# Layer 2's exponentials and piece scalings pinned to source order on ScalarE, reciprocal rows kept through SyncE's queue

## The chip, the cores and the metric

The kernel runs on one core of a Trainium2 chip. The metric is the device time of one launch in microseconds (us); the time before is the median of three runs. Engines carry the names of the profile: PE is TensorE (PEld its weight loads), DVE VectorE, ACT ScalarE, POOL GpSimd, SP SyncE. A q behind a name (SPq, ACTq, POOLq) is the sequencer of that engine, which waits and issues transfers. L967 is line 967 of the kernel.

## The reference, cut to what matters

Four layers follow each other on `x` of shape (4, 512, 32, 32): four images, 512 channels, 1024 positions. Each layer is `x = x + layer(groupnorm(x))`. Layers 0 and 3 (attention with mixed heads, and a memory read with the top 8 of 2048 items) are not touched. Layer 1 is a gate for each channel. Layer 2, which the change touches, is plain attention with eight heads of 64:

```python
def _L2_conv_ref(x, Wq, bq, Wkv, bkv, Wp, bp):
    q = _conv1x1(x, Wq, bq)
    kv = _conv1x1(x, Wkv, bkv)
    k, v = jnp.split(kv, 2, axis=1)
    q, k, v = (t.reshape(b, NUM_HEADS, D_K, l) for t in (q, k, v))   # shortened
    attn = jnp.einsum('bhct,bhcs->bhts', q, k) * SCALE
    attn = jax.nn.softmax(attn, axis=-1)
    out = jnp.einsum('bhts,bhcs->bhct', attn, v)
    out = _conv1x1(out.reshape(b, c, h, w), Wp, bp)
    return out

# --- layer 1 ---
x = x + _L1_conv_ref(_gn(x), ...)        # a gate for each channel of each image
# --- layer 2 ---
x = x + _L2_conv_ref(_gn(x), L2_conv_Wq, L2_conv_bq, L2_conv_Wkv, L2_conv_bkv, L2_conv_Wp, L2_conv_bp)
```

The kernel computes the softmax without taking off a maximum. Every reciprocal of a sum of exponentials is kept, and at the end of the kernel all of them are tested against two bounds; if one lies outside, a slower general path computes the result again.

## The kernel before, the parts concerned

The language places instructions by a scheduler that works with a model of their durations: an instruction without a mark goes where the model finds its inputs ready and its engine free, even far ahead of its place in the source. The kernel's helper `pin` takes that freedom away for one instruction: it goes behind whatever was written last for the same engine.

```python
    def pin(ins):
        return tc.keep_in_program_order(ins)
```

Layer 2 works in units. A unit is a pair of heads `m`, a half of the queries `n` and four of the eight tiles of keys: 16 units for an image, 64 in all. `scores2` multiplies keys by queries into PSUM (L973), ScalarE takes the exponentials (L967), and `apply2` multiplies the unit before with its values (L1006). The exponentials are added up on GpSimd (L987, L991) and VectorE (L992).

```python
    def scores2(b, u, before=None):
        ...
        def exp2():
            e = places2[:, count[0] % 6]
            count[0] += 1
            nc.scalar.activation(e, scs[len(es)], AF.Exp)                 # L967
            es.append(e)

        for i, t in enumerate(range(t0, t0 + 4)):
            sc = ps_s.tile([P, 2, NB], F32, tag="sc", ...)                # three such buffers
            for r in range(2):
                pin(nc.tensor.matmul(sc[:, r, :], ...k..., ...q..., start=True, stop=True))  # L973
            scs.append(sc)
            if before is None or i < 2:
                exp2()
        if before is not None:
            apply2(b, before, exp2)      # values of the unit before; takes the other two exp2 inside
        ...
        nc.gpsimd.tensor_add(I["es", m, n], es[0], es[1])                 # L987, first half of the keys
        ...
            nc.gpsimd.tensor_add(two, es[i], es[i + 1])                   # L991
            nc.vector.tensor_add(I["es", m, n], I["es", m, n], two)       # L992
```

When both halves of the keys are done, `finish2` sums the exponentials over the partitions by a matmul with ones, takes the reciprocal and scales the output. The last two lines keep one row of reciprocals for each of the two heads, for the test at the end.

```python
    def finish2(b):
        ...
            pin(nc.tensor.matmul(rsp[r * HD:(r + 1) * HD, :], ones[:, 0:HD], es[:, r, :], ...))   # L1027
        ri = apool.tile([P, NB], F32, tag="rb", bufs=2, name=f"ri_{nm}")
        nc.scalar.copy(ri, rsp)                                           # L1032
        nc.vector.reciprocal(ri, ri)                                      # L1033
        nc.vector.tensor_mul(I["o"][:, m, n * NB:(n + 1) * NB], pv, ri)   # L1034
        for r in range(2):
            i = 2 * ((b * KC + m) * (T // NB) + n) + r
            nc.gpsimd.dma_start(out=seen[i:i + 1, :], in_=ri[r * HD:r * HD + 1])   # L1037
```

`put_out2` projects the output of an image and adds the image itself, gated by layer 1. That image lies in DRAM; eight pieces of it (`xr`, 128 x 512, in two buffers) are loaded, scaled by ScalarE, added to the projection by VectorE and stored.

```python
    def put_out2(b):
        ...
        def add_out(m, ps):
            for n in range(T // NB):
                xr = apool.tile([P, NB], F32, tag="xr", bufs=2, name=f"xr_c{b}_{m}_{n}")
                nc.sync.dma_start(out=xr, in_=x1[b][:, m, n * NB:(n + 1) * NB])        # L1048
                nc.scalar.activation(xr, xr, AF.Identity,
                                     bias=I["tb"][:, m:m + 1], scale=s1[:, m:m + 1])   # L1049
                nc.vector.tensor_add(xr, ps[:, n * NB:(n + 1) * NB], xr)               # L1051
                nc.sync.dma_start(out=x2[b][:, m, n * NB:(n + 1) * NB], in_=xr)        # L1052
                nc.vector.bn_stats(st[:, n, :], xr)
        for m in range(KC):
            project(I["Wp"], tokens(I["o"]), m, None, lambda ps: add_out(m, ps), f"p2_{b}")   # matmuls at L197
```

Around an image the source says this:

```python
    scores2(0, UNITS2[0])
    for b in range(B):
        for s, u in enumerate(UNITS2):
            if s >= 1:
                scores2(b, u, UNITS2[s - 1])
            ...   # two steps of `behind` (layer 1's gate, norms) and of `ahead` (the next image), each unit
        ...       # take_q2 of the next image
        apply2(b, UNITS2[-1])
        ...       # take_k2
        finish2(b)
        ...       # take_v2
            scores2(b + 1, UNITS2[0])
        put_out2(b)
```

The gate of the last image is computed beside layer 2's first units. Some of its small steps go back and forth between TensorE and GpSimd:

```python
        def turned(l, products):
            products(ps)                               # small matmuls, pinned: L836, then L841 and L842
            take_small(u, ps[:, 0:KC])                 # ScalarE, L133
            yield
            for i in range(2):
                for n in range(2):
                    nc.gpsimd.tensor_scalar_mul(us[:, n], u, a_)                       # L829
                nc.gpsimd.tensor_sub(u_v[:, :, 0], cos_v[:, :, 0], sin_v[:, :, 1])     # L832
                nc.gpsimd.tensor_add(u_v[:, :, 1], cos_v[:, :, 1], sin_v[:, :, 0])     # L833
            return u
```

Of the kernel before, what the change touches and what calls it, by code (L numbers as in the profile page):

```python
# [11 lines left out]
AF = mybir.ActivationFunctionType  # L12
# [12 lines left out]
HD = C // NH  # L25
# [16 lines left out]
def fast_net(ctx: ExitStack, tc: tile.TileContext, a: dict, out: bass.AP, flag: bass.AP):  # L42
    nc = tc.nc
# [12 lines left out]
    def pin(ins):  # L56

        return tc.keep_in_program_order(ins)
# [21 lines left out]
    fcw, seen = both[0:NQ], both[HD:P]  # L80
# [5 lines left out]
    for i in range(P // NH):  # L86
        nc.scalar.dma_start(
            out=whp[i * NH:(i + 1) * NH], in_=a["w_head"].rearrange("r m g -> (r m) g")
# [13 lines left out]
        out=gavg_v, in_=gavg_v, compare_op=ALU.is_ge, fill=0.0, base=0,  # L102
# [3 lines left out]
        out=gavg_v, in_=gavg_v, compare_op=ALU.is_ge, fill=0.0, base=GSZ - 1,  # L106
# [81 lines left out]
    def tokens(src):  # L188
        return lambda k, n: src[:, k, n * NB:(n + 1) * NB]

    def project(w, rhs, m, at, evacuate, name="proj"):


        ps = place(at, f"{name}_{m}")
        for n in range(T // NB):
            for k in range(KC):
                pin(nc.tensor.matmul(  # L197
                    ps[:, n, :], w[:, k, m * P:(m + 1) * P], rhs(k, n),
                    start=(k == 0), stop=(k == KC - 1),
                ))  # L200
        evacuate(flat2(ps))
# [33 lines left out]
    e = apool.tile([P, 2, 2, 2, NK], F32, tag="e", name="e")  # L235
# [719 lines left out]
    def scores2(b, u, before=None):  # L955

        m, n, t0 = u
        I = img[b]  # L960
        nm = f"c{b}_{m}_{n}"
        es, scs = [], []

        def exp2():
            e = places2[:, count[0] % 6]
            count[0] += 1
            nc.scalar.activation(e, scs[len(es)], AF.Exp)  # L967
            es.append(e)

        for i, t in enumerate(range(t0, t0 + 4)):  # L970
            sc = ps_s.tile([P, 2, NB], F32, tag="sc", name=f"sc_{nm}_{t}")
            for r in range(2):
                pin(nc.tensor.matmul(  # L973
                    sc[:, r, :],
                    I["k"][r * HD:(r + 1) * HD, m, t * P:(t + 1) * P],
                    I["q"][r * HD:(r + 1) * HD, m, n * NB:(n + 1) * NB],
                    start=True, stop=True,
# [5 lines that stand above are left out]
            apply2(b, before, exp2)  # L983
        I["e", u] = list(es)
        if t0 == 0:
            I["es", m, n] = sums2[:, (2 * m + n) % 2]
            nc.gpsimd.tensor_add(I["es", m, n], es[0], es[1])  # L987
            es = es[2:]
        for i in range(0, len(es), 2):
            two = pair_sum[:, (t0 + i) // 2 % 2]  # L990
            nc.gpsimd.tensor_add(two, es[i], es[i + 1])  # L991
            nc.vector.tensor_add(I["es", m, n], I["es", m, n], two)  # L992

    def apply2(b, u, exp2=None):

        m, n, t0 = u
        I = img[b]
        if t0 == 0:
            finish2(b)
            I["pv", m, n] = ps_m.tile([P, NB], F32, tag="mm", name=f"pv_c{b}_{m}_{n}")  # L1000
        pv = I["pv", m, n]
        for i, e in enumerate(I.pop(("e", u))):
            t = t0 + i
            for r in range(2):
                h = 2 * m + r
                pin(nc.tensor.matmul(  # L1006
                    pv[r * HD:(r + 1) * HD, :], I["v"][:, t, h * HD:(h + 1) * HD],
                    e[:, r, :], start=(t == 0), stop=(t == TC - 1),
                ))
            if exp2 and i < 2:  # L1010
                exp2()
        if t0 == TC - 4:
            I["due"] = (m, n)

    def finish2(b):
        I = img[b]
        due = I.pop("due", None)
        if due is None:
            return
        m, n = due  # L1020
        nm = f"c{b}_{m}_{n}"
        if due == (0, 0):
            I["o"] = o_full.rearrange("p (k t) -> p k t", k=KC)
        es, pv = I.pop(("es", m, n)), I.pop(("pv", m, n))
        rsp = ps_s.tile([P, 2, NB], F32, tag="sc", name=f"rs_{nm}")[:, 0, :]
        for r in range(2):
            pin(nc.tensor.matmul(  # L1027
                rsp[r * HD:(r + 1) * HD, :], ones[:, 0:HD], es[:, r, :],
                start=True, stop=True,
# [4 lines that stand above are left out]
        nc.vector.tensor_mul(I["o"][:, m, n * NB:(n + 1) * NB], pv, ri)  # L1034
        for r in range(2):
            i = 2 * ((b * KC + m) * (T // NB) + n) + r
            nc.gpsimd.dma_start(out=seen[i:i + 1, :], in_=ri[r * HD:r * HD + 1])  # L1037

    def put_out2(b):
        I = img[b]  # L1040
        s1 = l2[b][1]
        mv = small.tile([P, KC, 2], F32, tag="mv", name=f"mv_d{b}")

        def add_out(m, ps):
            st = small.tile([P, 2, 6], F32, tag="bnst", name=f"st_d{b}_{m}")
            for n in range(T // NB):
                xr = apool.tile([P, NB], F32, tag="xr", bufs=2, name=f"xr_c{b}_{m}_{n}")
                nc.sync.dma_start(out=xr, in_=x1[b][:, m, n * NB:(n + 1) * NB])  # L1048
                nc.scalar.activation(  # L1049
                    xr, xr, AF.Identity, bias=I["tb"][:, m:m + 1], scale=s1[:, m:m + 1])  # L1050
                nc.vector.tensor_add(xr, ps[:, n * NB:(n + 1) * NB], xr)  # L1051
                nc.sync.dma_start(out=x2[b][:, m, n * NB:(n + 1) * NB], in_=xr)  # L1052
                nc.vector.bn_stats(st[:, n, :], xr)
            nc.vector.bn_aggr(mv[:, m, :], st.rearrange("p i s -> p (i s)"))

        for m in range(KC):
            project(I["Wp"], tokens(I["o"]), m, None, lambda ps: add_out(m, ps), f"p2_{b}")
        gc3 = const.tile([P, 2, KC], F32, tag=f"gc3_{b}", name=f"gc3_{b}")
        l3[b] = (mv, gc3)
# [247 lines left out]
    for b in range(B):  # L1307
# [22 lines left out]
        if not last:  # L1330
            for m in range(KC):
                take_k2(b + 1, m)
        finish2(b)
        if last:
            atts[0] = attention(*tiles[0])
# [745 lines left out]
```

## Time and profile before

| | before |
|---|---|
| time, median of 3 runs | 2743.99 us |
| lowest and highest | 2740.64 and 2755.8 us |
| span of the profiled run | 2741.6 us |
| mean granted TensorE clock | 0.980 |
| layer 2 in the profile | about 1373 to 2266 us |
| PE busy from 1590 to 1810 us | 217.44 of 220 us |
| ACT busy there | 77.56 us |
| POOL busy there | 93.16 us |
| DVE busy there | 89.71 us |

The first exponential of layer 2 starts at 1374.6 us and the last scaled piece (L1049) at 2266.1 us. In between one engine, PE, is busy nearly all the time, and the three others less than half of it. In such a stretch the time is made by what PE has to do and by the moments at which PE stands idle; the idle time of the other engines matters only where PE waits for it.

### The profile page before, as it was taken

How to read it: one execution, taken by the hardware profiler on the slowest of the kernel's cores; microseconds unless marked ns; L12 is line 12 of the kernel's file. 1: busy time of each engine (PE TensorE's matmuls, PEld its weight loads, DVE VectorE, ACT ScalarE, POOL GpSimd, SP SyncE). 2: the span in 40 equal slices, each digit the busy share in tenths (PEclk: the TensorE clock that was granted, in tenths of full speed). 3: DMA queues.
4: the chain of work that ended last, by engine and by line, in shares of the span. 5: the costliest groups of instructions: out<-in, count | busy, mean ns of one | idle time of the engine just before them, and what ended most of it. 6: DMA issues, size and time to landing. Idle time of an engine off the chain costs nothing.

```text
span 2741.6 us, 46996 instructions
## 1 busy us (share of the span) xinstructions
PE 2593.0 (95%) x18286; PEld 1180.3 (43%) x18286; DVE 1522.8 (56%) x2386; ACT 1007.6 (37%) x1149; POOL 1266.2 (46%) x1955
## 2 busy tenths in 40 slices
PE   8988999989989898989999999999999999999995
PEld 3443544545445444545433433343343334444442
DVE  5487337871588526873235224513623537788886
ACT  0565336551565426552154025214502622121210
POOL 2266325552455514653067017305702735666664
PEclk9999999999999999999999999999999999999997
DMA  2577438880687627785310030021002016767665
GB/s 78 128 206 204 128 93 219 218 216 28 172 216 202 164 69 193 205 207 199 116 32 1 31 123 1 16 77 62 1 31 92 1 48 189 220 186 216 185 183 148
DMA packets 159321, 349.82 MB, mean 128 GB/s; under 512 B 32361, under 2 KB 65129, under 8 KB 155378
## 3 DMA queue, kind: packets, MB, share of 16 engines
q1 hardware_dynamic: 86304, 167.04, 21.2%
q0 software_dynamic: 51200, 142.93, 19.3%
q10 hardware_dynamic: 21586, 36.76, 4.6%
q8 instruction: 147, 2.41, 0.4%
q14 instruction: 84, 0.69, 0.1%
HBM read 178.57 MB, written 33.69 MB: 77 GB/s over the span
## 4 chain that ended last, share of the span: by engine, by line
PE 82%; DMA 7%; ACT 4%; DVE 2%; issue 1%; POOL 1%; SPq 1%; ACTq 0%; POOLq 0%; DVEq 0%
PE at L1094 16%; PE sc_c L973 7%; PE pv_c L1006 7%; PE sc L451 7%; PE mx L197 7%; PE pv L511 6%; PE pt L410 4%; DMA s<-ss 4%; PE p L197 4%; PE sc L197 4%; PE v L209 3%; PE k L197 3%; PE q L197 3%; PE pt L684 3%; ACT ss L457 2%; PE mx L471 2%
## 5 line engine op out<-in xcount | busy, mean ns | idle before, releaser
L484 DVE STREAM_TRANSPOSE eT<-e 128x1024 f32<-128x1024 f32 x256 | 317.6, 1242 | 273.9 <-ACT e L478 272.0
L464 POOL DMA_DIRECT2D s<-ss x512 | 259.8, 515 | 384.4 <-ACT ss L457 299.6
L1111 POOL DMA_INDIRECT got<-in_mem,ix x256 | 280.2, 1095 | 208.3 <-DVE tmx L1117 92.3
L457 ACT COPY ss<-sc 128x1024 f32<-128x1024 f32 x256 | 258.9, 1011 | 264.4 <-PE sc L451 212.7
L967 ACT ACTIVATE eT<-sc_c 128x1024 f32<-128x1024 f32 x256 | 247.9, 1021 | 275.3 <-PE sc_c L973 213.3
L500 DVE BATCH_NORM_STATS2 st<-e 128x6 f32<-128x256 f32 x1024 | 341.6, 406 | 0.0
L451 PE MATMUL sc<-k,q 64*32 64x512 f32 x4096 | 287.1, 617 | 22.5 <-ACT ss L457 17.6
L991 POOL TENSOR_TENSOR e<-eT 128x1024 f32<-128x1024 f32 x96 | 231.3, 2412 | 164.7 <-ACT eT L967 133.2
L478 ACT ACTIVATE e<-mx 128x1024 f32<-128x1024 f32 x256 | 262.5, 1029 | 65.5 <-PE mx L471 28.0
L992 DVE TENSOR_TENSOR eT<-eT,e 128x1024 f32<-128x1024 f32 x96 | 132.8, 1384 | 274.0 <-POOL e L991 274.0
L511 PE MATMUL pv<-eT,v 128*64 128x128 f32 x4096 | 256.5, 279 | 0.0
L973 PE MATMUL sc_c<-q,k 64*128 64x512 f32 x1024 | 243.2, 614 | 11.3 <-ACT eT L967 9.0
L511 PEld LDWEIGHTS pv<-eT,v 128*64 128x64 f32 x4096 | 226.1, 139 | 63.9 <-issue 62.3
L1006 PE MATMUL pv_c<-eT,v 128*64 128x512 f32 x1024 | 234.4, 600 | 0.0
L471 PE MATMUL mx<-s,wmix 32*32 32x512 f32 x4096 | 159.6, 625 | 45.0 <-DMA s<-ss 44.9
L1135 DVE SCALAR_TENSOR_TENSOR acc<-got,et,acc 128x512 f32<-128x512 f32 x224 | 168.4, 752 | 8.0
L1033 DVE RECIPROCAL ri_c<-ri_c 128x512 f32<-128x512 f32 x32 | 107.0, 3345 | 96.1 <-ACT ri_c L1032 96.1
L973 PEld LDWEIGHTS sc_c<-q,k 64*128 64x128 f32 x1024 | 94.9, 189 | 144.0 <-issue 74.7
L1099 ACT COPY att<-at 128x1024 f32<-128x1024 f32 x64 | 64.8, 1012 | 217.8 <-PE at L1094 217.6
L987 POOL TENSOR_TENSOR eT<-eT 128x1024 f32<-128x1024 f32 x32 | 76.0, 2374 | 147.0 <-ACT eT L967 146.8
L587 POOL TENSOR_TENSOR o<-pv,rb 64x256 f32<-64x256 f32 x128 | 111.1, 868 | 67.1 <-ACT pv L574 60.2
L1006 PEld LDWEIGHTS pv_c<-eT,v 128*64 128x64 f32 x1024 | 70.9, 138 | 155.2 <-issue 154.6
(317 smaller groups left out, 3325.5 us busy)
## 6 DMA issues: line engine op xcount, KB each, us to landing
s<-ss SPq DMA_DIRECT2D x512, 128.0 KB
s<-ss POOLq DMA_DIRECT2D x512, 128.0 KB, 4.4
rb<-r POOLq DMA_DIRECT2D x64, 128.0 KB, 5.9
o<-o SPq DMA_DIRECT2D x32, 256.0 KB
xr<-in_x ACTq DMA_DIRECT2D x32, 256.0 KB
x<-xr SPq DMA_DIRECT2D x32, 256.0 KB
xr_c<-x SPq DMA_DIRECT2D x32, 256.0 KB
x<-xr_c SPq DMA_DIRECT2D x32, 256.0 KB
```

What stands on the lines that cost most here:

```text
L197: pin(nc.tensor.matmul(ps[:, n, :], w[:, k, m * P:(m + 1) * P], rhs(k, n), start=(k == 0), stop=(k == KC - 1),))
L451: pin(nc.tensor.matmul(sc[m * NS:(m + 1) * NS, r, :], q[r * HD:(r + 1) * HD, m, s * NS:(s + 1) * NS], k_[r * HD:(r + 1) * HD, m, n * NB:(n ...
L457: pin(nc.scalar.copy(ss[:, :, n * NB:(n + 1) * NB], sc))
L464: pin(relays[r].dma_start(out=s2[r * KC + m::NH], in_=ss[m * NS:(m + 1) * NS, r, :]))
L478: pin(nc.scalar.activation(e[:, half].rearrange("p r qq k -> p (r qq k)"), flat2(pairs[f"mx{half}"]), AF.Exp))
L484: pin(nc.vector.transpose(eT[:, j % 2].rearrange("p b (qq i r) x -> p i r qq b x", qq=2, i=4)[:, i, 2 * half:2 * half + 2], e[:, half].rea ...
L500: pin(nc.vector.bn_stats(st[:, i, 2 * half + r, qq, :], e[:, half, r, qq, :]))
L511: pin(nc.tensor.matmul(pv[r * HD:(r + 1) * HD, gp, :], I["v"][:, t, g * HD:(g + 1) * HD], eT[:, j % 2, t, :, 4 * g:4 * g + 4], start=(t == ...
L973: pin(nc.tensor.matmul(sc[:, r, :], I["k"][r * HD:(r + 1) * HD, m, t * P:(t + 1) * P], I["q"][r * HD:(r + 1) * HD, m, n * NB:(n + 1) * NB] ...
L1006: pin(nc.tensor.matmul(pv[r * HD:(r + 1) * HD, :], I["v"][:, t, h * HD:(h + 1) * HD], e[:, r, :], start=(t == 0), stop=(t == TC - 1),))
L1094: pin(nc.tensor.matmul(sc[:, n * NB:(n + 1) * NB], xn3[b][:, k, tt * P:(tt + 1) * P], memT[k][:, i0:i0 + NB], start=(k == 0), stop=(k == K ...
L1111: pin(nc.gpsimd.indirect_dma_start(out=got[:, i, :], out_offset=None, in_=a["mem"], in_offset=bass.IndirectOffsetOnAxis(ap=ix[:, i:i + 1], ...
```

## The change

The exponentials (L967) and the scalings of the pieces (L1049) are pinned: on ScalarE they now stand in the order of the source. The two transfers that keep a row of reciprocals each (L1037) are issued by SyncE instead of GpSimd. Nothing is computed differently. The first part is to keep the scalings, which wait for a transfer, from being placed ahead of exponentials that stand before them in the source; the second takes the wait for the reciprocal, and the issuing of 64 small transfers, out of GpSimd's stream.

```diff
         def exp2():
             e = places2[:, count[0] % 6]
             count[0] += 1
-            nc.scalar.activation(e, scs[len(es)], AF.Exp)
+            pin(nc.scalar.activation(e, scs[len(es)], AF.Exp))
             es.append(e)
...
         for r in range(2):
             i = 2 * ((b * KC + m) * (T // NB) + n) + r
-            nc.gpsimd.dma_start(out=seen[i:i + 1, :], in_=ri[r * HD:r * HD + 1])
+            nc.sync.dma_start(out=seen[i:i + 1, :], in_=ri[r * HD:r * HD + 1])
...
                 nc.sync.dma_start(out=xr, in_=x1[b][:, m, n * NB:(n + 1) * NB])
-                nc.scalar.activation(
-                    xr, xr, AF.Identity, bias=I["tb"][:, m:m + 1], scale=s1[:, m:m + 1])
+                pin(nc.scalar.activation(
+                    xr, xr, AF.Identity, bias=I["tb"][:, m:m + 1], scale=s1[:, m:m + 1]))
                 nc.vector.tensor_add(xr, ps[:, n * NB:(n + 1) * NB], xr)
```

## The prediction, made before the changed kernel ran

> **What bounds the kernel now.** I read the page first. PE is busy for 95% of the span and makes 82% of the chain that ended last; no other engine passes 56%.
>
> ```profile
> PE 2593.0 (95%) x18286; PEld 1180.3 (43%) x18286; DVE 1522.8 (56%) x2386; ACT 1007.6 (37%) x1149; POOL 1266.2 (46%) x1955
> ```
>
> The change touches layer 2 alone, so next I took the chain of waits in that stretch, in order of time (start, duration, work). It shows the pace that PE holds when nothing stops it:
>
> ```profile
> 1461.82 3.63 PE sc_c L973 x16
> 1465.45 3.58 PE pv_c L1006 x16
> ...
> 1478.09 3.63 PE sc_c L973 x16
> 1481.72 3.58 PE pv_c L1006 x16
> 1485.31 3.63 PE sc_c L973 x16
> 1488.94 1.01 PE rs_c L1027 x4
> 1489.95 3.43 PE pv_c L1006 x16
> ```
>
> Two units take 3.63 + 3.58 + 3.63 + 1.01 + 3.43 = 15.28 us, back to back. ScalarE has eight exponentials of 1.02 us (the group's mean is 1021 ns) in them, 8.2 us, so it keeps up with room. A gain in layer 2 can then only come from moments in which PE stands idle. The list of waits of PE there (1370 to 2275 us) is short; its columns are total us, times, longest:
>
> ```profile
> PE sc_c L973 <- ACT eT L967: 9.0, 4, 2.8
> PE amp L841 <- POOL amp L833: 4.3, 1, 4.3
> PE sc_c L973 <- DVE xr L650: 2.3, 1, 2.3
> ```
>
> Three causes and 15.6 us. The third is a piece of layer 0 that VectorE finishes before layer 2 begins, and the change doesn't reach it. The other two I followed in the timeline. The first kind, at an image's boundary:
>
> ```profile
> 1634.48 0.81 SPq L1048 DMA_DIRECT2D xr_c<-x  x2
> 1634.71 2.85 PE L973 MATMUL sc_c<-q,k 64*128 64x512 f32 x12
> 1637.64 1.52 ACT L1049 ACTIVATE xr_c<-xr_c,tb,s 128x512 f32<-128x512 f32 x2 [3.38 <-DMA xr_c<-x]
> 1639.06 1.91 ACT L967 ACTIVATE eT<-sc_c 128x1024 f32<-128x1024 f32 x2
> 1640.11 1.13 PE L973 MATMUL sc_c<-q,k 64*128 64x512 f32 x4 [2.56 <-ACT eT L967]
> ```
>
> The reader is to see that the two scalings at 1637.64 belong to the *next* image's output, 230 us too early. Their tile was free and their bias known, so the scheduler put them between exponentials. Their transfer was issued at 1634.48 only; ScalarE sat 3.38 us on it, the exponentials behind came late, no score buffer came free, and PE stood 2.56 us. The same happens near 1380, 1874 and 2110 us (gaps of PE 2.77, 2.65 and 1.05 us): once for each image.
>
> The second kind is on GpSimd:
>
> ```profile
> 1441.19 3.34 DVE L1033 RECIPROCAL ri_c<-ri_c 128x512 f32<-128x512 f32 x1
> 1442.25 0.57 POOL L829 TENSOR_SCALAR ampt<-amp,sincos 128x4 f32<-128x4 f32 x2
> 1447.76 1.10 POOL L1037 DMA_DIRECT2D fcw<-ri_c  x2 [4.94 <-issue]
> 1449.02 0.20 POOL L833 TENSOR_TENSOR amp<-ampt 128x2 f32<-128x2 f32 x1
> 1449.28 0.58 PE L841 MATMUL amp<-amp,turn 128*128 128x2 f32 x2 [4.32 <-POOL amp L833]
> ```
>
> GpSimd had two tiny steps left (L832, L833) at 1442.8, but two row transfers stood before them and waited for the reciprocal; PE waited for L833. Why the transfers began 3.2 us after the reciprocal's end (1444.53) the trace doesn't say.
>
> Each stop can cost more than its gap. Columns of the view by windows: stretch, length, five busy times, granted clock, DMA share, GB/s.
>
> ```profile
> 1450.00:1460.00 10.00, 10.00 (x37) 4.14 (x38) 1.41 (x2) 4.40 (x7) 9.70 (x16) 0.74 0.01 2
> 1460.00:1480.00 20.00, 20.00 (x110) 8.22 (x108) 11.53 (x8) 10.14 (x15) 15.00 (x13) 1.00 0.00 0
> ```
>
> After the 4.32 us gap the clock is 0.74, and the block of scores at 1450.72 took 5.86 us, not 3.63.
>
> **What the Trainium skill says.** "TensorE: Matmul & The Clock Gate", section "What's actually happening": an idle array drops to half its clock and comes back after a busy stretch of some 3.4 us; the window runs freely, so where a gap falls in it counts. The trace agrees in part: 0.74 after 4.32 us, 0.91 from 1880 to 1890 us after 2.65 us, but 1.00 after 2.56 us. "PSUM — Partial Sum Buffer", "Engine vs sequencer instructions": ScalarE, VectorE and GpSimd run their queues strictly in order. The trace agrees: ready exponentials sat behind L1049. "DMA: Bandwidth & Descriptors", "SWDGE vs HWDGE vs iDMA": descriptors of a transfer issued from GpSimd are made by GpSimd's own cores, those of SyncE by hardware. The trace has a median of 509 ns of GpSimd for each L1037.
>
> **Part one, the pins.** They remove four stops, one for each image. I add up, over each disturbed stretch, how far the starts of successive matmuls lie beyond the undisturbed pace (3.63 us for 16 of L973, 3.58 for 16 of L1006; the trace lists every start):
> - 1379.3 to 1389.8 us: 4.7 us (gap 2.8, the rest slow clock). Some of the slow clock comes from the 2.3 us wait for L650 just before and stays; I count 3.9.
> - 1634.7 to 1644.8: 2.9; I count 2.6, nearly the bare gap.
> - 1871 to 1892: 4.6 (gap 2.65, then the clock at 0.91); I count 4.2.
> - 2108 to 2119: 1.3; I count 1.2.
>
> Sum 11.9 us. The amounts shaved off allow for normal changes between kinds of matmul. The pins add no instruction. What they move: the two scalings of m = 0 now run in their own `put_out2`. At the boundary at 1600 us the four exponentials of the next image's first unit end at 1601.2; two scalings of 0.81 us end at 1602.8; VectorE needs them at 1607.0, when the first projection is done. Beside other work, cost 0. The remaining six keep their places: before, they ran at 1613 to 1628 us, in step with the 6.9 us of each projection.
>
> **Part two, the rows through SyncE.** Taken from GpSimd: 64 x 0.52 us = 33 us of issuing, and waits for the reciprocal of 210.6 us in all. Nearly all of this lies beside PE's work and is worth nothing. On the path is one case, the stop at 1444 us. From 1441.2 to 1456.5 us I find 7.0 us beyond the pace (4.3 gap, 2.2 in the slow block, about 0.5 in small matmuls). Without the transfers L833 would end near 1443.2, and PE asks for it at 1441.31 + 3.65 = 1444.96: 1.8 us in hand. I count 6.5 us. Added to SyncE: 64 issues of about 0.4 us (two took 0.81 above) on a queue nearly idle in layer 2; the rows land in 1.6 us (median of L1037) and are read at the kernel's end only.
>
> Sum: 11.9 + 6.5 = 18.4 us at most. The scheduler lays out all unpinned work anew, so a step of GpSimd may fall differently beside the gate's chain; I give the 6.5 three chances in four, minus 1.6. Another 0.8 goes for small new waits of exponentials behind small copies that they formerly passed. 18.4 - 1.6 - 0.8 = 16 us: 2744 - 16 = 2728.
>
> **Rivals.**
> 1. *The wait moves to the boundary.* In source order all eight scalings of an image stand before the exponentials of the next image's second unit, and each waits for load, add and store through two buffers. At the boundary above the last scaling ended at 1628.15 and the first score that needs ScalarE was exponentiated at 1628.73: 0.6 us in hand. If two more scalings in the row or a row transfer ahead on SyncE's queue delayed that chain by 2 us, three boundaries would lose 1.4 us each, some 4 us plus clock: 2732 to 2736. Against it: those six already stood there, and the m = 0 pieces have 4 us in hand.
> 2. *SyncE becomes the blocked queue.* It too runs in order; a row placed before its reciprocal ends holds up weight and image loads behind it, and a row stuck behind a weight load that waits for its buffer (one stood from 1568 to 1596 us) would hold a reciprocal's buffer, of which there are two, then L1032, then every exponential. That would cost PE tens of us: 2760 or more. For it: the scheduler misjudged the reciprocal on GpSimd already. Against it: that mistake was about 5 us, and the loads here are issued well ahead.
> 3. *The gate's chain stays late.* GpSimd's next large addition (2.35 us) could slide in ahead of L832. Then only the pins pay: 2732 to 2735.
> 4. *All idle time here is real, nothing new comes:* 2744 - 18.4, or 2725.6.
>
> **Range and chances.** Rivals 3 and 1 give 2732 to 2736, the full gain 2725 to 2726; the slow clock may depend on where a gap falls, some 4 us either way, and the runs before lie 4 below to 12 above their median. I take 2716 to 2742. 2% is 55 us, three times all the idle time found, so faster by over 2% gets 0.01; slower by over 2% needs rival 2 in its bad form: 0.02.
>
> **What would show it.** Right: PE's list of waits in layer 2 has no L973 <- ACT line above 1 us in all and no L841 line; L1049 runs in four groups of eight, none amid exponentials; L1037 stands on SPq; the two windows above stay at clock 1.00. The steps fail singly if the L841 wait stays (rival 3), if PE waits just after an image's last projection (rival 1), or if ACT waits at L1032 for a transfer (rival 2). Wrong altogether: a gain above 25 us, which would have to come from layer 3, or a loss.

## The result and the profile after

| | before | changed |
|---|---|---|
| time, median | 2744.06 us (6 runs) | 2718.7 us (6 runs) |
| lowest and highest | 2740.64 and 2755.8 us | 2710.27 and 2723.2 us |
| span of the profiled run | 2741.6 us | 2712.3 us |
| mean granted TensorE clock | 0.980 | 0.987 |

The ratio is 0.9896, with a 95% interval of 0.9872 to 0.992. The medians differ by 25.4 us (22 to 35 by the interval); 16 had been predicted. In layer 2 the mechanism held and one stop was counted too small; a further 4 us came from the end of the kernel, where the prediction had expected nothing.

The line of busy times of the changed kernel's page. PE works 15.7 us less by this count and GpSimd (POOL) 29 us less, and GpSimd has 64 instructions fewer:

```profile
PE 2577.3 (95%) x18286; PEld 1174.5 (43%) x18286; DVE 1514.7 (56%) x2386; ACT 1007.7 (37%) x1149; POOL 1237.2 (46%) x1891
```

The waits of PE in layer 2 of the changed kernel (total us, times, longest). The waits for exponentials and for L833 are gone; the piece of layer 0 (L650) is still waited for, and one small new wait has come:

```profile
PE sc_c L973 <- DVE xr L650: 2.3, 1, 2.3
PE gate L863 <- POOL zr L859: 0.7, 1, 0.7
```

The timeline at the first image's boundary, changed kernel. The two scalings of m = 0 stand in their own output, right behind the exponentials. In the changed profile the 32 scalings run in four groups of eight, with no exponential inside a group:

```profile
1580.98 3.77 ACT L967 ACTIVATE eT<-sc_c 128x1024 f32<-128x1024 f32 x4 [28.20 <-PE sc_c L973]
...
1584.61 1.53 ACT L1049 ACTIVATE xr_c<-xr_c,tb,s 128x512 f32<-128x512 f32 x2
```

The same boundary's end, ScalarE alone. The last scaling ends at 1611.79, and the next exponential, at 1612.28, waits for its scores and not for a transfer:

```profile
1610.98 0.81 ACT L1049 ACTIVATE xr_c<-xr_c,tb,s 128x512 f32<-128x512 f32 x1 [0.16 <-DMA xr_c<-x]
1612.28 1.94 ACT L967 ACTIVATE eT<-sc_c 128x1024 f32<-128x1024 f32 x2 [0.49 <-PE sc_c L973]
```

GpSimd in the gate's chain of the changed kernel. L832 and L833 now follow L829 within 0.3 us:

```profile
1440.17 0.56 POOL L829 TENSOR_SCALAR ampt<-amp,sincos 128x4 f32<-128x4 f32 x2
1440.70 0.20 POOL L157 TENSOR_TENSOR gsq_c<-gsq_c,mv 128x4 f32<-128x4 f32 x1
1440.85 0.19 POOL L832 TENSOR_TENSOR amp<-ampt 128x2 f32<-128x2 f32 x1
1441.00 0.19 POOL L833 TENSOR_TENSOR amp<-ampt 128x2 f32<-128x2 f32 x1
```

Windows of the changed kernel, columns as before; the clock (third number from the end) stays at 1.00:

```profile
1450.00:1460.00 10.00, 9.34 (x48) 3.85 (x46) 3.39 (x5) 4.84 (x7) 6.51 (x5) 1.00 0.00 0
1460.00:1480.00 20.00, 20.00 (x92) 7.07 (x88) 15.21 (x11) 11.44 (x14) 14.70 (x16) 1.00 0.01 1
```

**Where the time came from.** PE runs the same instructions in the same order in both kernels, so the starts of its matmuls cut both profiles into the same stages. Each row is the length of a stage in us, from one unit's first score (L973) to another's, with the units of an image counted from 1; the last row runs from the start of PE's last transpose (L1140) to the end. Two experiments told below, e1 and e2, stand beside:

| stage | before | changed | pins only (e1) | rows only (e2) |
|---|---|---|---|---|
| layers 0 and 1, to the first score of layer 2 | 1372.82 | 1369.23 | 1370.85 | 1375.58 |
| image 0, units 1 to 3 | 24.25 | 17.87 | 17.87 | 24.19 |
| image 0, units 4 to 13 | 88.17 | 81.66 | 88.66 | 81.71 |
| units 1 to 3 of image 1, with image 0's output between | 48.56 | 45.73 | 45.73 | 48.36 |
| the same, image 2 | 50.30 | 45.73 | 45.73 | 49.82 |
| the same, image 3 | 47.17 | 45.73 | 45.74 | 46.79 |
| end of the kernel | 14.21 | 10.19 | 14.26 | 10.09 |

Every stage left out agrees within 0.3 us in these four kernels. From before to changed, the rows below the first give 6.38 + 6.51 + 2.83 + 4.57 + 1.44 + 4.02 = 25.75 us, beside 25.4 us between the medians. The first row, 3.6 us, is not the change's doing: over all profiles of this study layer 2 began anywhere from 1369.2 to 1379.6 us.

Two of the rows had not been foreseen at their size: the first units, and the end. The end is a single instruction, the first drain of GpSimd after the last line of the program. Durations in ns, shortest, median and longest of three drains; before:

```profile
L2077 POOLq DRAIN  x3: 46/107/7915, 2732.9 to 2741.4; - x3
```

and changed:

```profile
L2077 POOLq DRAIN  x3: 40/107/3997, 2707.4 to 2712.0; - x3
```

All other engines wait for it: in before it ends at 2740.8 us (2732.9 + 7.9), and their last records follow from 2741.0 us on. In the changed kernel it is 3.92 us shorter.

### The profile page after: what moved, and what is told of

It is laid out like the page before. It is cut to its first block, busy times and chain, and to the rows that moved or that the text cites. A ratio compares the mean times of both kernels' runs of the same rounds, so it can differ in the third digit from the quotient of the medians.

```text
span 2712.3 us, 46987 instructions
## 1 busy us (share of the span) xinstructions
PE 2577.3 (95%) x18286; PEld 1174.5 (43%) x18286; DVE 1514.7 (56%) x2386; ACT 1007.7 (37%) x1149; POOL 1237.2 (46%) x1891
## 3 DMA queue, kind: packets, MB, share of 16 engines
q0 software_dynamic: 49152, 142.79, 19.4%
## 4 chain that ended last, share of the span: by engine, by line
PE 83%; DMA 6%; ACT 4%; DVE 3%; issue 1%; POOL 1%; SPq 1%; ACTq 0%; POOLq 0%; DVEq 0%
PE at L1094 16%; PE sc_c L973 8%; PE pv_c L1006 8%; PE sc L451 7%; PE mx L197 7%; PE pv L511 6%; DMA s<-ss 5%; PE pt L410 4%; PE p L197 4%; PE sc L197 4%; PE v L209 3%; PE k L197 3%; PE q L197 3%; ACT ss L457 3%; PE pt L684 3%; PE mx L471 2%
## 5 line engine op out<-in xcount | busy, mean ns | idle before, releaser
L967 ACT ACTIVATE eT<-sc_c 128x1024 f32<-128x1024 f32 x256 | 247.7, 1022 | 277.0 <-PE sc_c L973 213.8
L451 PE MATMUL sc<-k,q 64*32 64x512 f32 x4096 | 285.2, 613 | 20.5 <-ACT ss L457 15.7
L992 DVE TENSOR_TENSOR eT<-eT,e 128x1024 f32<-128x1024 f32 x96 | 131.5, 1370 | 247.3 <-POOL e L991 247.1
L973 PE MATMUL sc_c<-q,k 64*128 64x512 f32 x1024 | 237.0, 602 | 2.3 <-DVE xr L650 2.3
L973 PEld LDWEIGHTS sc_c<-q,k 64*128 64x128 f32 x1024 | 93.6, 186 | 130.8 <-issue 71.8
```

The costliest lines, as they stand in the source:

```text
L451: pin(nc.tensor.matmul(sc[m * NS:(m + 1) * NS, r, :], q[r * HD:(r + 1) * HD, m, s * NS:(s + 1) * NS], k_[r * HD:(r + 1) * HD, m, n * NB:(n ...
L973: pin(nc.tensor.matmul(sc[:, r, :], I["k"][r * HD:(r + 1) * HD, m, t * P:(t + 1) * P], I["q"][r * HD:(r + 1) * HD, m, n * NB:(n + 1) * NB] ...
```

## The experiments

Each time is a median, each ratio is against the kernel before on the same chip with its 95% interval; where a kernel was timed once there is no interval.

**e1, the pins without the rows.** The changed kernel with this undone:

```diff
-            nc.sync.dma_start(out=seen[i:i + 1, :], in_=ri[r * HD:r * HD + 1])
+            nc.gpsimd.dma_start(out=seen[i:i + 1, :], in_=ri[r * HD:r * HD + 1])
```

> Only the two pins; the rows of reciprocals stay with GpSimd. Theory (each part owns its stops): the four waits of PE for exponentials go, 6.4 + 2.8 + 4.6 + 1.4 = 15 us of layer 2 as the two profiles showed them, the wait at L841 of some 4 us stays, and GpSimd's last drain at the kernel's end stays near 7.9 us; the time is about 15 us under that of before. Rival (the surplus over the predicted 16 us is the run's own luck with the clock at layer 2's start and with the drain): 11 to 12 us under before, and the drain may be either 4 or 8 us.

Measured: 2732.13 us, ratio 0.9955 (0.994 to 0.997), 8 to 16 us under before's 2745.22. That interval does not tell the theory's 15 us from the rival's 11 to 12; the stages do: 6.38 + 2.83 + 4.57 + 1.43 = 15.2 us gained at the four stops, with the drain as in before. PE's waits:

```profile
PE amp L841 <- POOL amp L833: 4.3, 1, 4.3
PE sc_c L973 <- DVE xr L650: 2.3, 1, 2.3
```

The wait at L841 and the drain (7915 ns) are those of before to the digit. Which pin does it can be read from the compiled order of instructions: with the scalings alone pinned, ScalarE's order is that of the changed kernel; with the exponentials alone pinned, it is that of the kernel before. The pin on L967 has no effect here. The compiled orders also show that nothing else moved: PE and VectorE have the same order in before and changed, and GpSimd and SyncE too once the row transfers are left out.

**e2, the rows without the pins.** The kernel before with this:

```diff
-            nc.gpsimd.dma_start(out=seen[i:i + 1, :], in_=ri[r * HD:r * HD + 1])
+            nc.sync.dma_start(out=seen[i:i + 1, :], in_=ri[r * HD:r * HD + 1])
```

> Only the rows go through SyncE's queue; nothing is pinned. Theory: the four waits of PE for exponentials stay (about 9 us of gaps), the wait at L841 goes (6.5 us), and the last drain of GpSimd falls from 7.9 to about 4.0 us; about 10.5 us under before, so that the two parts add up to the whole change. Rival (the drain's length is luck and doesn't hang on the rows): 6.5 us under before, with a drain of either length.

Measured: 2736.51 us, ratio 0.9966 (0.9955 to 0.9977), 6 to 12 us under before, which holds both the theory's 10.5 and the rival's 6.5. By stage: 6.46 us in units 4 to 13, 4.12 at the end, about 1 us in small pieces at the four stops. The drain is 3997 ns, as in the changed kernel. The stops for exponentials stay:

```profile
PE sc_c L973 <- ACT eT L967: 9.7, 4, 4.6
PE sc_c L973 <- DVE xr L650: 2.3, 1, 2.3
PE gate L863 <- POOL zr L859: 0.7, 1, 0.7
```

So each part owns its stages, and by stages the two add up to the whole within about 1 us. The drain belongs to the rows and is not luck.

**e3, twice as many GpSimd transfers.** The kernel before with

```diff
-            nc.gpsimd.dma_start(out=seen[i:i + 1, :], in_=ri[r * HD:r * HD + 1])
+            for h in range(2):
+                nc.gpsimd.dma_start(
+                    out=seen[i:i + 1, h * NB // 2:(h + 1) * NB // 2],
+                    in_=ri[r * HD:r * HD + 1, h * NB // 2:(h + 1) * NB // 2])
```

> The kernel before, but each row of reciprocals is kept by two GpSimd transfers of 256 numbers, 128 transfers in place of 64. Theory (the last drain grows with the number of GpSimd transfers, 3.9 us for 64): a drain of about 12 us; with the doubled issuing ahead of L833 the wait at L841 grows by about 1 us; 4 to 6 us over before. Rival (the drain has two lengths, with or without rows on GpSimd, or one by chance): a drain of 8 or 4 us and a time within 2 us of before.

Measured: 2777.88 us, ratio 1.0122 (1.0099 to 1.0145), 33 us slower. Both expectations missed. The drain was 3832 ns, not 12 us, and 4.1 us less than in before; the stages from layer 2's first score to that drain lost about 34 us where some 1 us had been expected. PE's longest entry is new:

```profile
PE rs_c L1027 <- DVE eT L992: 20.9, 8, 9.4
```

One case in the timeline of e3 (L1038 is L1037 of before), by engine, is this:

```profile
1743.34 5.56 POOL L991 TENSOR_TENSOR e<-eT 128x1024 f32<-128x1024 f32 x2 [2.56 <-DVE eT L992]
1753.53 1.96 POOL L1038 DMA_DIRECT2D fcw<-ri_c  x4 [4.64 <-DVE ri_c L1033]
```

```profile
1749.90 3.34 DVE L1033 RECIPROCAL ri_c<-ri_c 128x512 f32<-128x512 f32 x1
1753.16 1.15 DVE L992 TENSOR_TENSOR eT<-eT,e 128x1024 f32<-128x1024 f32 x1
```

GpSimd stands 4.64 us for the reciprocal with additions behind it, and VectorE in turn has sums (L992) that need these additions. The transfers of three successive rounds begin at 1716.65, 1734.13 and 1753.53 us, 17.5 and 19.4 us apart, where PE needs 15.28 us for the same two units; so GpSimd falls behind PE until the sums for L1027 are late. At 1754.46 PE had waited 3.33 us for the L992 shown, which stood on VectorE behind the reciprocal. In before, with one transfer for each row, PE never waits at L1027. That this loop makes up all of the loss is argued, not shown.

**e4, half of the rows back to GpSimd.** The changed kernel with

```diff
-            nc.sync.dma_start(out=seen[i:i + 1, :], in_=ri[r * HD:r * HD + 1])
+            (nc.gpsimd if b < 2 else nc.sync).dma_start(
+                out=seen[i:i + 1, :], in_=ri[r * HD:r * HD + 1])
```

> The changed kernel, but the rows of images 0 and 1 (32 transfers) are again issued by GpSimd, those of images 2 and 3 by SyncE. Theory of a drain that grows with the number of GpSimd transfers: a drain near 6 us. Theory that it depends on whether the last layers hold such transfers: 4 us. Layer 2 at the pace of the changed kernel but for the wait at L841, which lies in image 0 and comes back with 4 to 6 us. In all 6 to 8 us over the changed kernel.

Measured: 2727.5 us, ratio 0.9935 (0.9914 to 0.9956). The drain was 5302 ns. Units 4 to 13 of image 0 took 90.4 us: the stop at L841 is back with its gap of 4.3 us, the wait at L863 grew to 1.6 us, and the stage lost 8.7 us where 4 to 6 were expected. The rest of layer 2 kept the changed kernel's pace. The expected 6 to 8 us over the changed kernel came to 8.8 between the medians and to 10 by stages (8.7 and 1.3 of the drain).

**e5, e6, e7: 16, 48 and 96 GpSimd transfers,** to see what the drain follows. e5 is e4 with `b < 1`, e6 with `b < 3`; e7 gives all rows to GpSimd, those of images 0 and 1 in halves.

> The changed kernel with the 16 row transfers of image 0 issued by GpSimd, the other 48 by SyncE. The last drain of GpSimd was 4.00 us with 0 such transfers, 5.30 with 32, 7.92 with 64, 3.83 with 128 short ones. Theory (the drain follows the number of transfers that GpSimd has issued, in steps of about 1.3 us, until it starts anew): 4.0 or 5.3 us. Rival (it follows which layer or image holds the last of them): with the last in image 0 it is 4.0 us, and the run with 48 shows the same as that with 32 or more.

> The changed kernel with the 48 row transfers of images 0 to 2 issued by GpSimd. Theory of the number: a drain between those of 32 and 64 transfers, 5.3 to 7.9 us, near 6.6. Rival of the place: 5.3 us as with 32, or 7.9 us.

> The changed kernel, but all rows by GpSimd, those of images 0 and 1 as two halves each: 96 transfers. Theory of the number that starts anew somewhere between 64 and 128: a drain of either above 7.9 us or below 4.0; a value between would speak against steps. Layer 2 is slowed in images 0 and 1 by GpSimd's in-order waits, as with 128 halves, where it lost 33 us in all, and about half as much here; images 2 and 3 hold the changed kernel's pace.

Timed once each: 2729.47, 2726.1 and 2736.62 us. In e7 layer 2 lost 10 us in image 1 (198.73 us from its fourth unit to the next image, where 188.69 is the rule) and, with the stop at L841, 7.7 us in units 4 to 13 of image 0, about the half of 33 us that was expected; images 2 and 3 held the pace. The drains of all these runs (at 96 and 128, 64 and 128 of the transfers are halves of a row):

| GpSimd transfers more than the changed kernel | 0 | 16 | 32 | 48 | 64 | 96 | 128 |
|---|---|---|---|---|---|---|---|
| first drain at the end, ns | 3997 | 4240 | 5302 | 6608 | 7915 | 1872 | 3832 |

The shortest of them, in e7:

```profile
L2080 POOLq DRAIN  x3: 46/107/1872, 2732.2 to 2734.6; - x3
```

From 32 to 64 the drain grows by 1306 and 1307 ns for 16 transfers; at 96 it is lower than with none. e6 hit its expected 6.6 us, and the rival of the place (which image holds the last transfer) is out: 48 is neither 32 nor 64. For 16 the expectation of whole steps was off (4.24, not 4.0 or 5.3).

**e8, 128 transfers through SyncE.** e3's halves, but in the changed kernel and issued by `nc.sync`.

> The changed kernel with each row kept by two SyncE transfers of 256 numbers, 128 in all. Theory (the 33 us that 128 GpSimd transfers cost are GpSimd's in-order stream, not the transfers themselves): layer 2 keeps the pace of the changed kernel within 1 us, and the last drain stays at 4.0 us. Rival (that many small transfers, or SyncE waiting for reciprocals ahead of its loads, slow layer 2 from any queue): PE waits of 10 us or more in layer 2.

Timed once: 2717.62 us. Every stage of layer 2 was within 0.1 us of the changed kernel's, and the drain 3997 ns. The loss of e3 came from GpSimd's stream, not from the transfers themselves, and SyncE's waits for reciprocals held up nothing. Whether GpSimd's issuing or its waiting weighs more was not separated.

**e9, the changed kernel once more,** unedited.

> The changed kernel once more, for its time and for what of its profile repeats. Theory (layer 2 and what follows are fixed, and the scatter of the runs lies in layers 0 and 1): from the first score of layer 2 to the end 1343 us as in the first profile, within 2 us; layer 2's start anywhere from 1369 to 1380 us; the time 25 us under before. Rival (the drain and the stages vary from run to run): a drain other than 4.00 us, or stages that differ by more than 2 us.

Measured: 2721.66 us, ratio 0.9906 (0.989 to 0.9922). Layer 2 began at 1377.15 us, 7.9 us later than in the first profile; every later stage repeated within 0.3 us, the drain to the digit (3997 ns). So the scatter of the runs sits in layers 0 and 1, and the stages compare kernels more sharply than the times do.

**e10, the scalings of image 0 alone pinned.** The kernel before with

```diff
-                nc.scalar.activation(
-                    xr, xr, AF.Identity, bias=I["tb"][:, m:m + 1], scale=s1[:, m:m + 1])
+                (pin if b == 0 else lambda ins: ins)(nc.scalar.activation(
+                    xr, xr, AF.Identity, bias=I["tb"][:, m:m + 1], scale=s1[:, m:m + 1]))
```

> The kernel before with the scalings of image 0 alone pinned; the exponentials unpinned, the rows with GpSimd. Theory (each stop stands by itself, and in the order of the compiled instructions only the two early scalings of image 0 move): the first three units take 17.9 us, or 19.5 if the clock falls after the wait for layer 0's last piece, in place of 24.2; the other three boundaries keep 48.4 to 50.3, 50, 47 us as in before; the wait at L841 stays, the drain is 7.92 us. Rival (the stops are linked, and PE's time lost at one is regained at the next): the later boundaries grow by what the first gains.

Timed once: 2745.09 us, with layer 2 beginning late at 1378.51. Units 1 to 3 took 19.47 us; the other boundaries 49.7, 50.1 and 46.7, together 146.5 where before had 146.0; the drain 7915 ns. What the first stop gave is not lost again at the later ones.

**e11, 32 more GpSimd transfers in layer 0.** The changed kernel with

```diff
-        pin(nc.gpsimd.dma_start(out=rows, in_=ri[0:NS]))
+        for h in range(2):
+            w = slice(h * NS // 2, (h + 1) * NS // 2)
+            pin(nc.gpsimd.dma_start(out=rows[w], in_=ri[w]))
```

> The changed kernel, but the 32 small GpSimd transfers of layer 0 that store reciprocals (32 x 32) are each issued in two halves: 32 more GpSimd transfers, all over a millisecond before the end. Theory (the last drain follows the number of GpSimd transfers over the whole kernel): a drain other than 4.00 us, near 5.3 as with 32 rows. Rival (only transfers of layer 2 or later count): 4.00 us as in the changed kernel.

Timed once: 2718.79 us, and the drain is that of 32 rows within 2 ns:

```profile
L2079 POOLq DRAIN  x3: 40/107/5304, 2710.9 to 2716.8; - x3
```

The drain follows the number of GpSimd transfers in the whole kernel, not their bytes (halves of the same rows were sent) nor their place: these lay over a millisecond before it. Nor is it the length of GpSimd's instruction stream: e11 has 2808 GpSimd records in its trace and e4, with the same number of transfers, 2868; the drains are 5304 and 5302 ns.

## Why the prediction fell short

Two steps failed. "Nearly all of this lies beside PE's work and is worth nothing" left out the end of the kernel, where the transfers taken from GpSimd were worth 4.0 us. And in part one the first stop was counted at 3.9 us and measured 6.38.

- **The bound.** Right for layer 2, which was PE's pace plus its stops; with the stops gone, its stages in the changed kernel repeat within 0.1 us (first profile and e9). It was not the bound of the last 10 us of the kernel, which no term covered.
- **Part one, three of its four terms.** Right in kind and slightly small: counted 2.6, 4.2 and 1.2, measured 2.83, 4.57 and 1.44 us. What had been read from the trace, 2.9, 4.6 and 1.3, was within 0.15 us; the amounts shaved off had no ground. One reading was off without effect: the scalings at 1637.64 ran about 200 us too early, not 230, for VectorE takes these pieces at 1844.3 us.
- **Part one, the first stop: a term that failed.** "Some of the slow clock comes from the 2.3 us wait for L650 just before and stays; I count 3.9." It was 6.38. The clock in short windows shows two slow stretches. First two lines of before, then one of the changed kernel:

```profile
1373.25:1376.67 3.42, 3.42 (x10) 1.63 (x8) 0.60 (x4) 1.45 (x2) 0.00 (x0) 0.50 0.96 338
1383.49:1386.91 3.42, 3.42 (x10) 1.09 (x10) 1.23 (x1) 0.99 (x2) 2.02 (x2) 0.50 0.00 0
1373.25:1376.67 3.42, 3.42 (x18) 1.37 (x16) 0.00 (x0) 2.80 (x4) 3.42 (x2) 1.00 0.53 165
```

  The stretch behind L650 ended at 1376.67, before the window that was counted began (1379.3). The slow clock inside that window, from 1383.49 on, followed the stop's own gap and went with it, so the 0.8 us shaved off was wrong. The other 1.7 us is the stretch behind L650. The chain of waits of the kernel *before*, which had not been read at this place, shows what it cost there:

```profile
1371.32 5.82 DMA x<-xr
...
1377.15 2.98 DMA xr_c<-x
...
1380.93 0.81 ACT xr_c L1049
1381.74 0.92 ACT eT L967
...
1382.71 3.05 PE sc_c L973 x8
1385.75 4.17 PE pv_c L1006 x16
```

  The scaling waited for a load, the load for the store of layer 0's last piece. That chain fixed when PE went on; how fast PE had run before was hidden under it and cost nothing. In e2 the first 24 scores ran quicker and the gap grew to match, 4.55 us in place of 2.77, and the stage was as long (24.19 against 24.25):

```profile
1375.58 5.42 PE L973 MATMUL sc_c<-q,k 64*128 64x512 f32 x24 [2.31 <-DVE xr L650]
1385.55 3.49 PE L973 MATMUL sc_c<-q,k 64*128 64x512 f32 x8 [4.55 <-ACT eT L967]
```

  Without the scaling the chain of the changed kernel goes straight on:

```profile
1369.23 7.14 PE sc_c L973 x32
1376.36 3.58 PE pv_c L1006 x16
```

  Whether the slow stretch behind L650 comes is luck of the run: with the early scalings gone the stage took 17.87 us in e1, e4, e8, e9, e11 and the changed kernel, and 19.5 to 19.6 in e5, e6, e7 and e10. So the term is 6.4 us without that stretch and 4.7 with it; 1.7 of the 6.38 us were the luck of the profiled run.
- **Part two, the stop at L841.** Right: counted 6.5, measured 6.51, and 6.46 alone in e2. The new wait of 0.7 us at L863 is within it. On SyncE each issue took 0.58 us (median), not the 0.4 counted, at no cost.
- **Part two, what was left out: the other step that failed.** The sum looked at layer 2 alone and had no term for the end of the kernel. The number of GpSimd transfers also sets the drain there, which no engine's work covers: 7.92 us with the 64 rows on GpSimd, 4.00 without them. This is the largest single piece of the miss. Why the drain depends on that number stays open.
- **The discounts.** The 2.4 us taken off for a new layout of GpSimd's stream and for exponentials behind small copies paid for nothing: GpSimd's other work kept its order, and e1 and the changed kernel show no such loss.
- **The sum.** 16 + 2.4 (discounts) + 2.5 (first stop) + 0.8 (the other three) + 4.0 (end) = 25.7 us.
- **The rivals.** The first did not come: the last scaling at the boundary has 0.49 us in hand, and no boundary lost time. The second neither: L1037 stands on SyncE's queue and no one waits for it (e8 doubles it at no cost). The third neither: L833 ended at 1441.19 with no wait behind it.
- **The signs.** All that were named for a right picture came: no wait of L973 for ScalarE and none at L841, scalings in groups of eight, the rows on SyncE's queue, the two windows at clock 1.00. They see layer 2 only and could not show the drain. "A gain above 25 us, which would have to come from layer 3" was the mark for a wrong picture. The medians passed it by 0.4 us, well within the noise; the 4 us that had not been foreseen came not from layer 3's work but from the drain behind it.

## What to carry to other kernels

When an engine's stop is taken away, cost it by what ends it. If a transfer chain ends it, the chain fixes the length of the stage, and the work beside the chain is hidden; so compare the stage, from the chain's start on, with what the engine needs for its work alone (24.2 against 17.9 or 19.5 us here), and not with the gap (2.8 us). An instruction that waits for a transfer is worth pinning behind the work that doesn't, when the scheduler's model may take the transfer as landed; pin that instruction alone and look at the compiled order to see which pin acts. And look at the kernel's last microseconds for engines whose drain hangs on how they were used.

## What the runs showed of the hardware that was not expected

- The first drain of GpSimd at the end took 1.87 to 7.92 us, the same within 2 ns for kernels with the same number of GpSimd transfers (3997 in e2, e8, e9 and the changed kernel, 7915 in before, e1 and e10). It follows the number of transfers that GpSimd issued in the whole launch: 82 ns for each between 32 and 64 extra ones, but only 15 ns for each from 0 to 16, and 1.87 us in all at 96. What in the machine it waits for is open.
- A stop of PE of 2.3 us (L650) was followed by half the clock for 3.4 us in some runs of equal instructions (before, e5, e10) and by none in others (e2, the changed kernel). The Trainium skill, "TensorE: Matmul & The Clock Gate", section "What's actually happening", has the activity window run freely, which would fit this scatter, though no run here shows the window. It also says that the clock drops after at least one idle window of some 3.4 us; here gaps of 2.3 and 2.65 us were enough. The scatter was worth 0 or 1.6 to 1.7 us of the stage.
- GpSimd's in-order stream was nearer to the edge than its 46% of busy time suggests: 64 transfers more, some 31 us of issuing (64 x 0.49), made the kernel 33 us slower (e3), while the same 128 transfers on SyncE's queue cost nothing (e8). That the two figures are alike is no proof that issuing is the cause.
